# One root for the last two slabs of a two-layer graph network, and what is left on GpSimd at its end

## The chip, the cores and the metric

The kernel runs on one core of a Trainium2 chip. The metric is the time of one execution on the device in microseconds; a version is given by the median of its runs.

## The reference

The input is x (4096 x 64) and a sparse 0/1 matrix adj (4096 x 4096). Two graph layers follow one another, each inside a residual layer normalization:

```python
# layer 0: the last 100 neighbours of a row, each weighted by 0.5**(its rank from the end)
support = x @ weight
rank = jnp.cumsum(mask, axis=1); deg = rank[:, -1:]
k = jnp.minimum(deg, 100.); pos = rank - (deg - k)
w = mask * jnp.where(pos > 0, 0.5 ** (k - pos), 0.0)
x = _layernorm(x + w @ support + bias)

# layer 1: mean over neighbours and self, linear, relu, division by the row's length
deg = jnp.clip(jnp.sum(adj, axis=1, keepdims=True) + 1.0, 1.0, None)
z = jnp.concatenate([x, (adj @ x + x) / deg], axis=1) @ W + b
out = jax.nn.relu(z)
out = out / jnp.maximum(jnp.linalg.norm(out, axis=1, keepdims=True), 1e-12)
x = _layernorm(x + out)
```

`_layernorm` subtracts a row's mean and divides by sqrt(variance + 1e-5). That last division, in layer 1, is the place of the change.

## The kernel before, in words

**Tiles.** The 4096 rows are cut into eight slabs of 512 rows (g = 0 to 7; L = 7 is the last), and a slab into TB = 4 blocks of 128 rows, one row to a partition. A row statistic of a slab is a tile of 128x4, the rows' 64 features a tile of 128x256. The matrix comes in 64 pieces of 512 KB, loaded by GpSimd's DMA queue along with 16 smaller loads of x; SyncE's queue carries the weights and the eight stores of the result, one for each slab.

**Stages.** Up to about 205 us TensorE counts, weighs and sums layer 0 and, as soon as slabs of its result are there, sums parts of layer 1. From L756 on the order is written out by hand, call by call: the scheduler is manual, so each engine executes its instructions in the order in which the Python code emits them. The calls named `own` and `own_half` are what is left of TensorE's sums; the calls named `last_...`, `offset` and `store` are the epilogue of layer 1 for a unit of slabs (u6, u45, u01, u2, u3; the last slab comes in two halves u7b and u7a, and as u7 when they are joined).

**The epilogue of a unit**, in its order of data:

- `last_pz`, `last_z`, `last_relu`, `last_sq`, `last_ss`: the linear map, relu, and sums of squares;
- `last_rn` (with `last_sn` ahead of it for the halves of slab 7), `last_y`, `last_add`: division by the length and the residual;
- `last_mv`: mean and variance of each row (bn_stats and bn_aggr on VectorE);
- the root r = (variance + eps)^-0.5, in one of two forms. With a `last_s` ahead, `last_r` takes `root_b`: ScalarE has made s = sqrt(v + eps) (L358), VectorE refines it and inverts it with four small instructions (L364, L365, L367, L368). Without, `last_r` takes `root_p`: GpSimd adds eps (L376) and raises to -0.5 (L378);
- `offset`: off = -mean * r, on VectorE in one instruction (L735) for the first form, on GpSimd in two (L737, L738) for the second;
- `last_o`: y * r + off for each block of 128 rows, by ScalarE (L745, needs off), or (y - mean) * r by VectorE (L747, doesn't need off);
- `store`: SyncE's DMA (L754), which waits for the unit's normalizations.

Before the change only slab 7 has the first form. Slab 3's root and offset are GpSimd's last four instructions; slab 3's four blocks are normalized by ScalarE and stored, while slab 7's are shared: two by VectorE, two by ScalarE after slab 3's, and stored last. Slab 7's two halves write their moments into one tile, `mv_7` (128x4x2).

After the last instruction of each engine come closing ones that the kernel doesn't spell out: SyncE waits for the stores' semaphores, each engine executes a DRAIN, and a barrier over all engines (EVENT_SEMAPHORE) ends the program. The profile books them on L959, the line that builds the program.

Of the kernel before, what the change touches and what calls it, by code (L numbers as in the profile page):

```python
# [9 lines left out]
F32 = mybir.dt.float32  # L10
# [13 lines left out]
P = 128  # L24
R = 512
TB = R // P
# [13 lines left out]
def adj_resnorm_kernel(  # L40
# [23 lines left out]
    nc = tc.nc  # L64
# [11 lines left out]
    small = ctx.enter_context(tc.tile_pool(name="small", bufs=5))  # L76
# [276 lines left out]
    ep = {}  # L353

    def root_a(v, eps, name):

        s = small.tile([P, v.shape[1]], F32, tag="s", name=f"s_{name}")
        nc.scalar.activation(s, v, AF.Sqrt, bias=eps)  # L358
        return s

    def root_b(s, v, eps, name):

        q = small.tile([P, v.shape[1]], F32, tag="q", name=f"q_{name}")
        nc.vector.tensor_tensor(q, s, s, ALU.mult)  # L364
        nc.vector.scalar_tensor_tensor(q, q, eps, v, ALU.add, ALU.add)  # L365
        r = small.tile([P, v.shape[1]], F32, tag="r", name=f"r_{name}")
        nc.vector.reciprocal(q, q)  # L367
        nc.vector.scalar_tensor_tensor(r, s, 2.0, q, ALU.mult, ALU.mult)  # L368
        return r

    def root_p(v, eps, name, tag):

        n = v.shape[1]
        r = small.tile([P, n], F32, tag=tag, name=f"{tag}_{name}")
        if eps:
            nc.gpsimd.tensor_scalar(r, v, eps, None, ALU.add)  # L376
            v = r
        nc.gpsimd.tensor_tensor(r, v, power[:, 0:n], ALU.pow)  # L378
        return r

    def moments(y, name, mv=None):
        n = y.shape[1]
        st = small.tile([P, n, 6], F32, tag="st", name=f"st_{name}")
        if mv is None:
            mv = small.tile([P, n, 2], F32, tag="mv", name=f"mv_{name}")
        for t in range(n):
            nc.vector.bn_stats(st[:, t, :], y[:, t, :])
        for t in range(n):
            nc.vector.bn_aggr(mv[:, t, :], st[:, t, :])
        return mv  # L390
# [191 lines left out]
    L = NG - 1  # L582
# [55 lines left out]
    def unit(*slabs):  # L638
        name, bs = "_".join(map(str, slabs)), [g * TB + t for g in slabs for t in range(TB)]
        n = len(bs)  # L640
        tiles = []
        for i in range(n // TB):
            tiles.append(a16p.tile([P, 4 * TB // n, n, D], F32, tag="a16", name=f"u_{name}_{i}"))
        four = [t[:, i] for t in tiles for i in range(4 * TB // n)]
        return name, bs, four
# [51 lines left out]
    def last_y(u):  # L697
        name, bs, (z, _, y, _) = u
        rn = ep["rn", name].unsqueeze(2).to_broadcast([P, len(bs), D])
        nc.vector.scalar_tensor_tensor(y, z, 0.0, rn, ALU.max, ALU.mult)  # L700
# [3 lines left out]
        engine = nc.gpsimd if len(bs) >= TB else nc.vector  # L704
        engine.tensor_tensor(y, y, x1[:, rows(bs), :], ALU.add)

    mv_7 = small.tile([P, TB, 2], F32, tag="mv_7", name="mv_7")

    def last_mv(u):
        name, bs, (_, _, y, _) = u  # L710
        if len(bs) < TB:
            ep["mv1", str(L)] = mv_7
            t = bs[0] - L * TB
            moments(y, f"l1_{name}", mv_7[:, t : t + 2, :])
        else:
            ep["mv1", name] = moments(y, f"l1_{name}")

    def last_s(u):
        name = u[0]
        ep["s1", name] = root_a(ep["mv1", name][:, :, 1], eps_ln, f"l1_{name}")  # L720

    def last_r(u):
        name = u[0]
        v = ep["mv1", name][:, :, 1]
        if ("s1", name) in ep:
            ep["r1", name] = root_b(ep["s1", name], v, eps_ln, f"l1_{name}")
        else:
            ep["r1", name] = root_p(v, LN_EPS, name, "r1")

    def offset(u):  # L730
        name, bs, _ = u
        mv, r = ep["mv1", name], ep["r1", name]
        off = ep["off", name] = small.tile([P, len(bs)], F32, tag="off", name=f"off_{name}")
        if ("s1", name) in ep:
            nc.vector.scalar_tensor_tensor(off, mv[:, :, 0], -1.0, r, ALU.mult, ALU.mult)  # L735
        else:
            nc.gpsimd.tensor_tensor(off, mv[:, :, 0], r, ALU.mult)  # L737
            nc.gpsimd.tensor_scalar(off, off, -1.0, None, ALU.mult)  # L738

    def last_o(u, t0, t1, engine=nc.scalar):  # L740
        name, bs, (_, _, y, o) = u
        mv, r, off = ep["mv1", name], ep["r1", name], ep["off", name]
        for t in range(t0, t1):
            if engine is nc.scalar:
                engine.activation(o[:, t, :], y[:, t, :], AF.Identity, bias=off[:, t : t + 1], scale=r[:, t : t + 1])  # L745
            else:
                engine.tensor_scalar(  # L747
                    o[:, t, :], y[:, t, :], mv[:, t, 0:1], r[:, t : t + 1], ALU.subtract, ALU.mult
                )

    def store(u):
        name, bs, (_, _, _, o) = u
        for i, b in enumerate(range(0, len(bs), TB)):
            nc.sync.dma_start(out=out[bs[b] // TB], in_=o[:, b : b + TB, :])  # L754
# [46 lines left out]
    last_pz(u01)  # L801
    last_z(u45)
    last_mv(u6)
    last_relu(u45)
    last_sq(u45)
# [15 lines left out]
    u2 = unit(2)  # L821
    last_pz(u2)
    last_o(u6, 2, 4)
    last_o(u6, 0, 2)
    last_y(u45)
    last_rn(u01)
# [13 lines left out]
    own(3, 5)  # L840
    last_add(u01)
    last_mv(u45)
    own_half(1, 1)
    own_half(1, 4)
# [7 lines left out]
    u3 = unit(3)  # L852
    last_pz(u3)
    last_mv(u01)
    half_hT(1)
    u7 = unit(L)
# [14 lines left out]
    last_r(u01)  # L871
    own_half(0, 0)
    last_o(u45, 4, 6)
    last_ss(u3)
    own_half(0, 3)
# [27 lines left out]
    last_rn(u7a)  # L903
    offset(u2)
    last_o(u01, 6, 8)
    last_r(u3)
    last_y(u7a)
    last_add(u7a)
    last_o(u2, 0, 2)
# [1 line left out]
    last_mv(u7b)  # L911
    last_o(u2, 2, 4)
    last_mv(u7a)
    offset(u3)
    last_s(u7)
    store(u2)
    last_o(u3, 0, 2)
    last_r(u7)
    last_o(u3, 2, 4)
    offset(u7)  # L920
    last_o(u7, 2, 4, nc.vector)
    last_o(u7, 0, 2, nc.scalar)
    store(u3)
    store(u7)


_INS = ["x", "x_quads", "adjT", "weights"]
# [36 lines left out]
```

## Time and profile before

| what | us |
|---|---|
| time before, median of 3 runs (lowest, highest) | 243.77 (243.39, 243.98) |
| span of the profiled execution, first to last instruction | 241.5 |
| the runs' times less that span | 1.9 to 2.5 |
| TensorE busy in the span | 209.5 (87%) |
| VectorE busy | 175.7 (73%) |
| ScalarE busy | 135.4 (56%) |
| GpSimd busy | 92.8 (38%) |
| last ACTIVATE of ScalarE ends, from the span's start | 236.2 |
| last store issued | 236.25 |

The profile lists the span of the profiled execution, and no total for it apart from the runs' times; the last row but one and the last come from the timeline. A busy share is an average over the whole span, and in the last 10 us TensorE has nothing left to do, so the shares say little of the stage in which the change lies. The lines that matter are those of the timeline of that stage, of the chain of waits and of the closing instructions.

### The profile page before, as it was taken

Reading aid. Unit: us, or ns where it says so; the run is one execution under the profiler, and the core shown is the slowest. Engines: PE = TensorE matmul, PEld = TensorE weight load, DVE = VectorE, ACT = ScalarE, POOL = GpSimd, SP = SyncE. Lnnn points to the kernel's source line nnn. Section 1 sums busy time; section 2 is a strip of 40 time slices with the busy share of each in tenths; the row PEclk is TensorE's granted clock in tenths of the full one; section 3 lists DMA queues with packets and bytes.
Section 4 is the critical chain, followed back from the end, with each engine's and each line's share of the span. In section 5 each row is a group of like instructions: output and inputs, shape, how many; then the busy total and the mean of one; then the engine's idle time right before and its main releaser. Section 6 shows DMA issues by size and latency. Waiting matters only on the chain.

```text
span 241.5 us, 7394 instructions
## 1 busy us (share of the span) xinstructions
PE 209.5 (87%) x3123; PEld 95.2 (39%) x3167; DVE 175.7 (73%) x451; ACT 135.4 (56%) x203; POOL 92.8 (38%) x172
## 2 busy tenths in 40 slices
PE   8885679989699999999999999999999999996800
PEld 2222224333323442443345334433453454765700
DVE  5665677996488689579756975597559765789980
ACT  5375667787367647665555465555644521171691
POOL 8664588136106302133212421243161000287960
PEclk9999999999889999999999999999999999999975
DMA  5999999999999999999899999999970000000031
GB/s 92 185 227 247 247 224 210 216 225 213 212 226 214 212 217 220 212 214 216 145 174 176 196 184 185 186 191 188 197 146 3 3 0 0 3 18 6 0 109 43
DMA packets 11456, 37.33 MB, mean 155 GB/s; under 512 B 1568, under 2 KB 2720, under 8 KB 11424
## 3 DMA queue, kind: packets, MB, share of 16 engines
q0 software_dynamic: 9984, 35.66, 74.3%
q1 hardware_dynamic: 1440, 1.21, 1.5%
q8 instruction: 24, 0.39, 0.6%
q14 instruction: 8, 0.07, 0.1%
HBM read 69.37 MB, written 1.05 MB: 292 GB/s over the span
## 4 chain that ended last, share of the span: by engine, by line
PE 50%; DMA 21%; POOL 11%; DVE 8%; ACT 4%; issue 4%; POOLq 0%; ACTq 0%; DVEq 0%
PE acc L305 14%; PE acc_part L314 13%; DMA a<-in_adjT_dram 10%; PE v L278 6%; DMA x<-in_x_dram 6%; DMA c<-in_x_quads_dram 5%; PE cnt L248 4%; PE v L287 4%; ACT w L294 3%; POOL r L378 3%; POOL a L104 2%; PE va L314 2%; DVE w L295 2%; PE pz L414 2%; PE rep L266 1%
## 5 line engine op out<-in xcount | busy, mean ns | idle before, releaser
L294 ACT ACTIVATE w<-v,less 128x1024 int16<-128x1024 f32 x64 | 71.3, 1114 | 54.3 <-PE v L287 42.1
L295 DVE TENSOR_SCALAR w<-v 128x1024 int16<-128x1024 f32 x64 | 78.3, 1223 | 23.7 <-PE v L287 22.4
L305 PE MATMUL acc<-w,xhl 128*128 128x512 bf16 x236 | 66.0, 383 | 2.7 <-issue 1.4
L104 POOL DMA_DIRECT2D a<-in_adjT_dram x64 | 35.3, 554 | 80.3 <-PE acc_part L314 37.2
L314 PE MATMUL acc_part<-a,x1hl 128*128 128x512 bf16 x135 | 37.1, 381 | 1.9 <-issue 1.4
L305 PEld LDWEIGHTS <-xhl 128*128 128x128 f16 x256 | 23.1, 98 | 35.3 <-issue 11.5
L314 PEld LDWEIGHTS <-x1hl 128*128 128x128 f16 x224 | 18.6, 98 | 30.6 <-issue 13.4
L278 PE MATMUL v<-a,tri 32*32 32x512 bf16 x1024 | 29.5, 388 | 0.7 <-ACT w L294 0.6
L248 PE MATMUL cnt<-a,pick 128*32 128x512 bf16 x256 | 21.8, 387 | 8.6 <-DMA a<-in_adjT_dram 8.0
L258 DVE TENSOR_TENSOR cs<-cnt,cs 128x512 bf16<-128x512 f32 x27 | 18.5, 684 | 13.4 <-PE cnt L248 13.4
L287 PE MATMUL v<-near,mine 32*32 32x512 bf16 x1024 | 28.2, 379 | 0.0
L268 ACT ACTIVATE near<-rep,most 128x512 bf16<-128x512 f32 x35 | 23.9, 683 | 5.2 <-PE rep L266 5.1
L278 PEld LDWEIGHTS <-tri 32*32 32x32 bf16 x1024 | 9.8, 88 | 22.0 <-issue 21.3
L378 POOL TENSOR_TENSOR rn<-ss,power 128x4 f32<-128x4 f32 (+1 forms) x5 | 6.3, 1275 | 25.9 <-DVE ss L683 25.8
L266 PE MATMUL rep<-cs,further 128*128 128x512 bf16 x35 | 13.5, 386 | 1.9 <-DVE cs L258 1.5
L238 POOL TENSOR_TENSOR x<-x,wts 128x256 f32<-128x256 f32 x8 | 5.8, 728 | 24.3 <-DMA x<-in_x_dram 24.3
L248 PEld LDWEIGHTS <-pick 128*32 128x32 bf16 x256 | 5.0, 93 | 22.8 <-DMA a<-in_adjT_dram 12.6
L233 POOL TENSOR_TENSOR a<-a,ident_b 128x128 bf16<-128x128 bf16 x32 | 12.8, 433 | 0.1
L745 ACT ACTIVATE u<-u,off,r 128x64 f32<-128x64 f32 x28 | 10.0, 427 | 0.3 <-POOL off L738 0.3
L287 PEld LDWEIGHTS <-mine 32*32 32x32 bf16 x1024 | 9.7, 88 | 1.2 <-issue 1.0
L661 PE MATMUL va<-wts,hT 128*128 128x64 f32 x64 | 8.0, 276 | 2.4 <-DVE hT L629 1.9
L670 ACT ACTIVATE u<-u 128x256 f32<-128x256 f32 (+1 forms) x5 | 2.5, 502 | 12.4 <-DVE u L666 12.4
(136 smaller groups left out, 245.0 us busy)
## 6 DMA issues: line engine op xcount, KB each, us to landing
a<-in_adjT_dram POOLq DMA_DIRECT2D x64, 512.0 KB, 10.8
c<-in_x_quads_dram POOLq DMA_DIRECT2D x8, 128.0 KB, 11.6
x<-in_x_dram POOLq DMA_DIRECT2D x8, 128.0 KB, 8.6
out_dram<-u SPq DMA_DIRECT2D x8, 128.0 KB, 1.7
wts<-in_weights_dram SPq DMA_DIRECT2D x1, 160.0 KB, 7.4
touch<-in_x_quads_dram SPq DMA_DIRECT2D x1, 0.5 KB, 1.6
```

The source lines that it names most:

```text
L104: nc.gpsimd.dma_start(out=a, in_=adjT[g, k])
L248: nc.tensor.matmul(cnt[g][quarters[q], :], lhsT=pick[:, PW - 4 * k : PW - 4 * k + Q], rhs=A[g][k][:, q, :], start=first, stop=last,)
L258: nc.vector.tensor_tensor(new, cnt[g], cs[g], ALU.add)
L266: nc.tensor.matmul(pr, lhsT=further, rhs=cs[g], start=True, stop=True)
L268: nc.scalar.activation(near[g], pr, AF.Relu, bias=most, scale=-1.0)
L278: nc.tensor.matmul(v[e // 2][quarters[q], e % 2, :], lhsT=tri[quarters[e], :], rhs=A[g][k][quarters[e], q, :], start=True, stop=False,)
L287: nc.tensor.matmul(v[e // 2][quarters[q], e % 2, :], lhsT=mine[quarters[e], 4 * k + q, :], rhs=nr[quarters[e], :], start=False, stop=True,)
L294: nc.scalar.activation(w[:, 0:2, :], v[0], AF.Relu, bias=less)
L295: nc.vector.tensor_scalar(w[:, 2:4, :], v[1], -STEP * MAX_NEIGH, 0.0, ALU.add, ALU.max)
L305: nc.tensor.matmul(acc0[g], lhsT=xhl[:, b, :], rhs=w[:, q, :].bitcast(BF16), start=(k, q) == (NK - 1, 0), stop=(k, q) == (0, KB - 1),)
L314: nc.tensor.matmul(acc, lhsT=x1hl[:, b, :], rhs=A[g][b // KB][:, b % KB, :], start=first, stop=last)
L378: nc.gpsimd.tensor_tensor(r, v, power[:, 0:n], ALU.pow)
```

## The change

Slab 3's root is taken out of GpSimd and made together with slab 7's. `mv_7` becomes `mv_37`, with columns 0 to 3 for slab 3 and 4 to 7 for slab 7; a joint unit `u37` carries `last_s`, `last_r` and `offset` once over 128x8. Four GpSimd instructions (L376, L378, L737, L738 for slab 3) are gone. Each of the two slabs is then normalized half by VectorE and half by ScalarE, slab 7 ahead of slab 3, and stored in that order.

```diff
-    mv_7 = small.tile([P, TB, 2], F32, tag="mv_7", name="mv_7")
+    mv_37 = small.tile([P, 2 * TB, 2], F32, tag="mv_37", name="mv_37")
+    slot_of = {3: 0, L: TB}
 
     def last_mv(u):
         name, bs, (_, _, y, _) = u
-        if len(bs) < TB:
-            ep["mv1", str(L)] = mv_7
-            t = bs[0] - L * TB
-            moments(y, f"l1_{name}", mv_7[:, t : t + 2, :])
+        if bs[0] // TB in slot_of:
+            ep["mv1", "37"] = mv_37
+            t = slot_of[bs[0] // TB] + bs[0] % TB
+            moments(y, f"l1_{name}", mv_37[:, t : t + len(bs), :])
         else:
             ep["mv1", name] = moments(y, f"l1_{name}")
...
     def last_o(u, t0, t1, engine=nc.scalar):
         name, bs, (_, _, y, o) = u
-        mv, r, off = ep["mv1", name], ep["r1", name], ep["off", name]
+        if bs[0] // TB in slot_of:
+            n0 = slot_of[bs[0] // TB]
+            mv, r, off = [ep[what, "37"][:, n0 : n0 + TB] for what in ("mv1", "r1", "off")]
+        else:
+            mv, r, off = ep["mv1", name], ep["r1", name], ep["off", name]
...
     last_o(u01, 6, 8)
-    last_r(u3)
     last_y(u7a)
...
     last_mv(u7a)
-    offset(u3)
-    last_s(u7)
+    u37 = ("37", u3[1] + u7[1], None)
+    last_s(u37)
     store(u2)
-    last_o(u3, 0, 2)
-    last_r(u7)
-    last_o(u3, 2, 4)
-    offset(u7)
+    last_r(u37)
+    offset(u37)
     last_o(u7, 2, 4, nc.vector)
     last_o(u7, 0, 2, nc.scalar)
+    store(u7)
+    last_o(u3, 2, 4, nc.vector)
+    last_o(u3, 0, 2, nc.scalar)
     store(u3)
-    store(u7)
```

## The prediction

> **What bounds the kernel now.** I read the busy slices first, then the chain of waits, then the timeline of the last 10 us, and last the instructions of L959, the line that launches the program and to which its closing instructions are booked. The busy slices show TensorE at 0 in the last two of 40 (each 6.04 us), so from about 229 us the time belongs to the epilogue of layer 1. All instructions of the change lie there. The chain of waits runs through GpSimd until 234.10 (offset of slab 3), then ScalarE's normalizations to 236.22, and stops. The span ends at 241.5: 5.3 us after the last compute are not in that chain. The timeline shows both edges of the computation (columns: start, us, engine, line, operation, tiles, count):
>
> ```profile
> 232.13 0.23 POOL L376 TENSOR_SCALAR r<-mv_l 128x4 f32<-128x4 f32 x1
> 232.45 1.04 POOL L378 TENSOR_TENSOR r<-r,power 128x4 f32<-128x4 f32 x1
> 233.57 0.20 POOL L737 TENSOR_TENSOR off<-mv_l,r 128x4 f32<-128x4 f32 x1
> 233.78 0.30 ACT L358 ACTIVATE s_l<-mv,eps_ln 128x4 f32<-128x4 f32 x1
> 233.86 0.24 POOL L738 TENSOR_SCALAR off<-off 128x4 f32<-128x4 f32 x1
> 234.13 1.43 ACT L745 ACTIVATE u<-u,off,r 128x64 f32<-128x64 f32 x4
> 234.97 0.16 DVE L735 SCALAR_TENSOR_TENSOR off<-mv,r_l 128x4 f32<-128x4 f32 x1
> 235.05 0.53 DVE L747 TENSOR_SCALAR u<-u,mv,r_l 128x64 f32<-128x64 f32 x2
> 235.47 0.76 ACT L745 ACTIVATE u<-u,off,r_l 128x64 f32<-128x64 f32 x2
> ```
>
> ScalarE is ready at 234.08 (end of the root s_l) and GpSimd's offset at 234.10, so neither holds the other by more than 0.03 us. ScalarE ends at 235.47 + 0.76 = 236.23 and SyncE issues the last store at 236.25. What follows, from L959 in the windows 236.5 to 238.3, 238.3 to 239.5 and 240.7 to 240.9 (durations in ns: shortest/median/longest, then first and last start):
>
> ```profile
> L959 SPq EVENT_SEMAPHORE  x9: 17/28/28, 236.6 to 238.3; - x9
> L959 POOLq DRAIN  x1: 6902/6902/6902, 233.8 to 233.8; - x1
> ...
> L959 SPq DRAIN  x2: 7/7/7, 238.4 to 238.5; - x2
> ...
> L959 POOLq EVENT_SEMAPHORE  x2: 17/17/17, 240.8 to 240.8; - x2
> ```
>
> SyncE has waited for every store and is through at 238.46. Then nothing runs until 240.7 except one thing: GpSimd's closing DRAIN, begun at 233.81 (as GpSimd's last instruction was under way) and 6.90 us long, to 240.71. The closing barrier (GpSimd's EVENT_SEMAPHORE) starts 0.05 us later, and 0.75 us after that the span is over. **So the end is not set by the last store but by GpSimd: its last instruction ends at 234.10, plus 6.61 us of DRAIN.** SyncE has 2.25 us to spare.
>
> **What the Trainium skill says.** "Perfetto Trace Analysis", section "Sequencer-only Instruction (DRAIN, etc)", says that the profiler shows such an instruction from the moment its semaphores are satisfied; so the 6.90 us aren't a semaphore wait. The trace agrees in kind for ScalarE: its closing DRAIN starts at 235.2, takes 1.077 us and ends with its last ACTIVATE. "VectorE: DVE Perf Modes", section "The DRAIN you can't avoid", calls the closing DRAINs a constant of about 12 ns on all engines; this trace differs, 6902 ns on GpSimd, and the measurement decides. "DMA: Bandwidth & Descriptors", section "SWDGE vs HWDGE vs iDMA", says that DMAs issued from GpSimd have their descriptors made by software on its cores, and those from SyncE by hardware. All 80 loads here are GpSimd's (64 + 8 + 8 in the list of issues), all stores SyncE's. A tail that clears up after 80 DMAs would be 6.61 / 80 = 83 ns for each, my estimate from this trace; it would have nothing to do with the stores. No page gives its length.
>
> **The change part by part.**
>
> *GpSimd loses slab 3's root and offset:* L376 (0.23), L378 (1.04), L737 (0.20) and L738 (0.24), with gaps 232.06 to 234.10 = 2.04 us at the end of its queue. Nothing takes their place; its last instruction becomes slab 2's L738 (231.82 + 0.24 = 232.06). What comes before it is unmoved. With the DRAIN unchanged it ends at 232.06 + 6.61 = 238.67 in place of 240.71.
>
> *The root on ScalarE and VectorE becomes 128x8.* It replaces one of 128x4 at the same place in both queues and waits for the same last moments (slab 7, first half, done 233.75), since slab 3's moments are done by 231.47. ScalarE's Sqrt stays 233.78 to about 234.08. On VectorE five small instructions carry twice the columns. Nearest rows: L364 took 0.127 at 128x2 and 0.153 at 128x4, so about +0.05 for four columns more; L367 0.17 and 0.18, +0.02; L365 and L368 the same at both sizes, +0.01 each, and the offset +0.01. Sum +0.10. From below 0 (pipelining hides it), from above +0.25 (each grows as L364). I take +0.10: the offset ends at 235.13 + 0.10 = 235.23.
>
> *Order of the normalizations.* ScalarE did slab 3 (4) from 234.13 while VectorE made slab 7's root, then slab 7 (2). Now it has only 2 + 2 and all wait for the offset: it idles from 234.08 to 235.23 + 0.04 = 235.27 (0.04 is what passed from VectorE's ss_7a to ScalarE's root). Four ACTIVATEs start 0.34, 0.33 and 0.33 apart (six took 2.10 from 234.13 to 236.23), the last takes 0.42: end 236.70. Before: 236.23. **Price +0.47 us** on the way to the last store. VectorE's two added normalizations cost 2 x 0.22 and end at 235.15 + 3 x 0.22 + 0.31 = 236.12, before ScalarE; nothing is behind them.
>
> *Stores.* The same two DMAs in the other order. Slab 7's is issued when ScalarE has done its two, at 235.27 + 0.34 + 0.42 = 236.03, and occupies SyncE's queue for 0.33 (the duration of each issue) until 236.36; slab 3's follows at 236.72. They don't collide; before they stood at 235.59 and 236.25. Landing 1.7 us after issue (from the list of issues) is kept, so SyncE is through at 238.46 + 0.47 = 238.93.
>
> *VectorE and GpSimd's contention.* "SBUF — State Buffer", section "SBUF: two separate sides", says that GpSimd and VectorE share a port pair as an exclusive lock. The trace shows it: L677 at 128x128 took 0.757 while GpSimd's 128x256 add ran (229.29) and 0.292 otherwise. Does VectorE gain where GpSimd falls quiet, 232.06 to 234.10? Its L700 there took 0.292, as without GpSimd at 228.1: gain 0. In reverse the DRAIN now begins while VectorE still works, 4 us instead of 1.8; what that costs isn't shown; 0 to 1 us, I take 0 since its 6.9 us aren't tensor work, and keep 1 us for the range.
>
> *Sum.* The barrier starts after the later of GpSimd's DRAIN (238.67) and SyncE (238.93), plus about 0.05: 238.98 in place of 240.76. That is **-1.78 us**: 2.04 us freed on GpSimd, of which the last 0.26 are lost because the stores are late next. Span 241.50 - 1.78 = 239.72. The median shown, 243.77, stands 2.27 above the profiled span; I carry that over: **241.99, say 242.0 us**.
>
> **Rivals.**
>
> *The DRAIN has its fixed length after GpSimd's last instruction (forecast).* For: no semaphore wait in it, nothing else runs in its last 2.25 us, and ScalarE's and VectorE's DRAINs end with their own last work. Against: there is one such DRAIN in the trace, so a fixed length can't be told from a fixed end. 242.0; with 1 us more of DRAIN it ends at 239.67 and the time is 242.7. Chance 0.83.
>
> *The DRAIN ends with the stores.* It would last until a fixed time after the last store is in (240.71 - 238.46 = 2.25 after SyncE is through), whatever GpSimd did before. Then freeing GpSimd brings nothing and the late last store shows in full: +0.47, 244.2, slower by 0.19%, inside what can't be told from no change. It decides as soon as the DRAIN end moves with SyncE and not with GpSimd. Chance of this and of a DRAIN that grows to eat nearly all of the gain: 0.13.
>
> *The tail grows by more than the gain.* The same tie to the stores, with a root or a store that is later than worked out by 0.3 us or more: +0.25 from the root's upper bound, and VectorE slowed by the concurrent DRAIN. 244.6. For it: the 0.757 of L677. Against: VectorE's L735 and L747 already ran beside the DRAIN at 0.16 and 0.308, as L441's same shape elsewhere (0.307). Chance 0.04.
>
> That the change doesn't do what it says is no rival: GpSimd's list loses exactly the four instructions.
>
> **How the numbers follow.** A measurement here tells about 0.3% (0.73 us) from no change. The forecast's cases from -2.0 (root costs nothing and ScalarE starts sooner, so that the DRAIN alone decides: 238.67, -2.04) to -1.05 all lie beyond it: faster 0.83. Same 0.13, slower 0.04. Predicted 242.0. The range reaches from 241.5 (-2.04 and run-to-run 0.2) to 243.0 (the DRAIN 1 us longer and 0.3 of spread); the two tied cases are left out, together under 0.2.
>
> **What would show it.** Right: GpSimd's DRAIN starts near 231.8, lasts about 6.9 and ends near 238.7; the barrier starts right after SyncE's last DRAIN, near 238.9; ScalarE's last ACTIVATE ends near 236.7, 0.47 later than before. Wrong: a DRAIN that begins at 231.8 and still ends 2.2 us after SyncE's, so over 8.9 us long. The root's step is wrong if slab 7's offset ends after 235.4, the store's if the two issues stand within 0.4 us.

## The result, and the profile after

| | before | changed |
|---|---|---|
| median, us (22 runs each) | 243.69 | 242.34 |
| lowest, us | 242.75 | 241.33 |
| span of the profiled execution, us | 241.5 | 239.5 |

The ratio of the two is 0.9946, with a 95% interval of 0.9923 to 0.997: the changed kernel is faster by 0.5%, about 1.3 us.

The timeline of the changed kernel near its end (start, us, engine, line, operation):

```profile
231.64 0.24 POOL L739 TENSOR_SCALAR off<-off 128x4 f32<-128x4 f32 x1
...
233.28 0.30 DVE L389 BATCH_NORM_AGGREGATE mv<-st_l_7a 128x2 f32<-128x6 f32 x2
233.61 0.30 ACT L358 ACTIVATE s_l<-mv,eps_ln 128x8 f32<-128x8 f32 x1
233.94 0.17 DVE L364 TENSOR_TENSOR q_l<-s_l 128x8 f32<-128x8 f32 x1 [0.37 <-ACT s_l L358]
...
234.84 0.17 DVE L736 SCALAR_TENSOR_TENSOR off<-mv,r_l 128x8 f32<-128x8 f32 x1
234.93 0.98 DVE L752 TENSOR_SCALAR u<-u,mv,r_l 128x64 f32<-128x64 f32 x4
235.04 1.43 ACT L750 ACTIVATE u<-u,off,r_l 128x64 f32<-128x64 f32 x4 [1.13 <-DVE off L736]
```

GpSimd's last instruction is now slab 2's and ends at 231.88. ScalarE stands idle for 1.13 us behind the joint root's offset, which the last line shows in brackets, and ends at 235.04 + 1.43 = 236.48 (the times are rounded). The closing instructions, booked on L963 here, in the windows 236 to 238.3, 238.3 to 238.7 and 238.7 to 239.1:

```profile
L963 POOLq DRAIN  x1: 6902/6902/6902, 231.6 to 231.6; - x1
...
L963 SPq EVENT_SEMAPHORE  x6: 28/28/28, 238.3 to 238.6; - x6
...
L963 SPq DRAIN  x2: 7/7/7, 238.7 to 239.0; - x2
L963 POOLq EVENT_SEMAPHORE  x2: 17/17/17, 238.7 to 238.8; - x2
```

GpSimd's DRAIN has the same length to the nanosecond, 6902 ns, and ends at 238.50. SyncE is through at 238.72, and the barrier begins at 238.74, right behind it. The bound has moved from GpSimd's DRAIN to the last store.

To compare executions that reach the epilogue at different times, I use one zero from here on: **the end of VectorE's last bn_aggr (L389)**, the last moments of slab 7. "Tail" is the time from there to the end of the span. SyncE is "through" when the last DRAIN that it executes ahead of the barrier has ended; "barrier" is the start of GpSimd's first EVENT_SEMAPHORE behind its DRAIN. All times below are in us from that zero:

| | GpSimd's last instruction ends | DRAIN ends | ScalarE ends | SyncE through | barrier | tail |
|---|---|---|---|---|---|---|
| before | 0.35 | 6.97 | 2.48 | 4.71 | 7.01 | 7.76 |
| changed | -1.69 | 4.93 | 2.90 | 5.14 | 5.17 | 5.91 |

The barrier starts behind the later of DRAIN and SyncE, and the tail ends 0.75 after it. The tail is 1.85 us shorter. The spans differ by 2.0; the rest, 0.17 us, is that the zero itself came earlier in this execution (233.57 from the span's start, 233.74 before).

### The profile page after: what moved, and what is told of

Same layout as the page of the kernel before. It is cut to its first block, busy times and chain, and to the rows that moved or that the text cites. A ratio compares the mean times of both kernels' runs of the same rounds, so it can differ in the third digit from the quotient of the medians.

```text
span 239.5 us, 7390 instructions
## 1 busy us (share of the span) xinstructions
PE 208.1 (87%) x3123; PEld 95.3 (40%) x3167; DVE 176.7 (74%) x453; ACT 134.6 (56%) x201; POOL 91.4 (38%) x168
## 3 DMA queue, kind: packets, MB, share of 16 engines
q0 software_dynamic: 9984, 35.66, 75.6%
## 4 chain that ended last, share of the span: by engine, by line
PE 49%; DMA 24%; DVE 12%; POOL 7%; ACT 3%; issue 3%; ACTq 0%; POOLq 0%; DVEq 0%
DMA a<-in_adjT_dram 24%; PE acc L305 13%; PE acc_part L314 13%; PE v L278 6%; PE cnt L248 4%; PE v L287 4%; ACT w L294 2%; PE va L314 2%; POOL a L104 2%; PE pz L414 2%; DVE st_l L387 2%; DVE w L295 1%; DVE u L700 1%; PE va L661 1%; PE vb L314 1%
## 5 line engine op out<-in xcount | busy, mean ns | idle before, releaser
L305 PE MATMUL acc<-w,xhl 128*128 128x512 bf16 x236 | 65.3, 379 | 2.5 <-issue 1.3
L378 POOL TENSOR_TENSOR rn<-ss,power 128x4 f32<-128x4 f32 (+1 forms) x5 | 6.3, 1275 | 27.6 <-DVE ss L683 27.5
L661 PEld LDWEIGHTS va<-wts,hT 128*128 128x128 f32 x64 | 7.6, 191 | 3.7 <-DVE hT L629 2.8
```

What stands on the lines that cost most here:

```text
L305: nc.tensor.matmul(acc0[g], lhsT=xhl[:, b, :], rhs=w[:, q, :].bitcast(BF16), start=(k, q) == (NK - 1, 0), stop=(k, q) == (0, KB - 1),)
L661: nc.tensor.matmul(pz[:, t, :], lhsT=h[:, ts(b % TB, P)], rhs=wn_sb, start=True, stop=True)
```

## The experiments

Theory A: GpSimd's closing DRAIN has a length of its own after GpSimd's last instruction. Theory B: it ends with the stores.

### e1: GpSimd's four instructions put back, for nobody

```diff
     last_o(u01, 6, 8)
+    spare_r = root_p(mv_37[:, 0:TB, 1], LN_EPS, "spare", "r1")
     last_y(u7a)
...
+    spare_off = small.tile([P, TB], F32, tag="off", name="off_spare")
+    nc.gpsimd.tensor_tensor(spare_off, mv_37[:, 0:TB, 0], spare_r, ALU.mult)
+    nc.gpsimd.tensor_scalar(spare_off, spare_off, -1.0, None, ALU.mult)
     u37 = ("37", u3[1] + u7[1], None)
```

> The changed kernel with four GpSimd instructions put back at the old place and of the old shapes (add of eps, power, product, sign, 128x4), into tiles that nobody reads; ScalarE, VectorE and the stores stay as changed. Theory A (GpSimd's DRAIN has a fixed length after its last instruction): GpSimd ends about 2.0 us later, its DRAIN of 6.90 ends about 7.0 us after VectorE's last bn_aggr, the time from that bn_aggr to the end of the span goes from 5.91 back to 7.76, and the time to that of the kernel before, about 243.7. Theory B (the DRAIN ends with the stores): the DRAIN starts later and is 2 us shorter, the tail stays at 5.9, the time at about 242.3.

Measured: median 243.83 (20 runs), ratio to before 1.0 (0.9974 to 1.0025). **The whole gain is gone, though nothing reads the four results and ScalarE ends (2.90) and SyncE is through (5.14) just where they were in the changed kernel.** The last GpSimd line of its timeline, and its DRAINs (its L967; the long one is the third duration, starting at 234.5):

```profile
234.56 0.24 POOL L921 TENSOR_SCALAR off_spare<-off_spare 128x4 f32<-128x4 f32 x1
...
L967 POOLq DRAIN  x3: 46/102/6902, 234.5 to 241.9; - x3
```

Again 6902 ns. B is refuted: SyncE was through at 5.14, as in the changed kernel, and the barrier waited until 6.43, 0.05 behind the end of the DRAIN. The tail is 7.17, not the 7.76 that A gave, because GpSimd ended 0.24 before the zero and not 0.35 after it; that gap is taken up below, with e9a.

### e2: the kernel before, without slab 3's root

```diff
-    last_r(u3)
+    ep["r1", "3"] = ep["r1", "2"]
...
-    offset(u3)
+    ep["off", "3"] = ep["off", "2"]
```

> The kernel before, with slab 3's root and offset left out and slab 2's used in their place (slab 3's result is then not the reference's). GpSimd's four instructions are gone, ScalarE's and VectorE's order is that of before, so the joint root's price is not paid. Theory A: DRAIN 6.90 long, ending 4.9 us after the last bn_aggr; SyncE is through 4.7 after it, so the DRAIN is last again and the tail is about 5.7 (0.2 shorter than the changed kernel's 5.91); time about 1.9 to 2.0 below before. Theory B: SyncE is where it was, so the DRAIN ends where it did, tail 7.76, time as before.

Measured: median 242.05, ratio to before 0.9932 (0.9912 to 0.9953). That is 1.7 us below the kernel before, where 1.9 to 2.0 were expected. Taking GpSimd's four instructions away is enough for the gain, without the joint root. DRAIN 6901 ns. The tail is 5.32, not 5.7: GpSimd ended 2.87 before the zero, so its DRAIN (over at 3.75) was hidden and SyncE (4.55) decided. SyncE's 4.55 against the changed kernel's 5.14 is the price of the joint root and its order: 0.59 us.

### e3: what the DRAIN's length depends on

```diff
-        nc.gpsimd.dma_start(out=x1[:, ts(g, TB), :], in_=x[:, ts(g, TB), :])
+        nc.scalar.dma_start(out=x1[:, ts(g, TB), :], in_=x[:, ts(g, TB), :])
```

> The kernel before, with the eight loads of x (128 KB each) issued from ScalarE's queue at the same places in the code, so that GpSimd issues 72 DMAs in place of 80 and 3% fewer bytes; all arithmetic stays. It asks what the length of the DRAIN depends on. If it clears up after each DMA at the estimated 83 ns: DRAIN 6.90 - 8 x 0.083 = 6.24 us, the tail 7.76 - 0.66 = 7.10, time about 243.0. If it goes by bytes: 6.7 and 7.56. If it is constant: 6.90 and 7.76. In each case eight issues of some 0.3 us lie on ScalarE, which waits for TensorE there, and should cost nothing.

Its DRAINs, and those of e5, which issues 104 DMAs from GpSimd:

```profile
L959 POOLq DRAIN  x3: 46/93/6249, 234.5 to 241.2; - x3
```

```profile
L965 POOLq DRAIN  x3: 46/102/8862, 234.1 to 244.0; - x3
```

With 72 DMAs the DRAIN is 6249 ns and the tail 7.09: the per-DMA estimate said 6240 ns and 7.10. The barrier followed the DRAIN (6.30) by 0.04, with the stores where they were (SyncE 4.71): a second refutation of B. The time, 243.47 with a ratio of 0.9987 (0.996 to 1.0014), neither confirms nor excludes a gain of 0.66 us. The profiled execution reached the zero at 234.41, the one of before at 233.74; whether eight issues on ScalarE cost something earlier wasn't separated.

### e5: the same bytes in more DMAs

```diff
-            nc.gpsimd.dma_start(out=a, in_=adjT[g, k])
+            for j in range(2 if g > 4 else 1):
+                half = slice(2 * j, 2 * j + 2) if g > 4 else slice(0, KB)
+                nc.gpsimd.dma_start(out=a[:, half, :], in_=adjT[g, k][:, half, :])
```

> The changed kernel with each of the 24 matrix loads of slabs 5, 6 and 7 issued as two DMAs of half the size, so GpSimd issues 104 DMAs in place of 80 and the same bytes. It asks whether the DRAIN goes by the number of DMAs. From the DRAINs measured at 72, 74 and 80 DMAs (6.249, 6.412, 6.902 us) a line of 0.0816 us for each DMA: 6.902 + 24 x 0.0816 = 8.86 us at 104, of which the end of the span pays all but what SyncE still covers (0.2 us): tail 5.91 + 1.7 = 7.6 us. If it goes by bytes, or the loads of x were special, 6.90 and 5.91.

DRAIN 8862 ns, against 8.86 us expected. The length goes by the number of DMAs that GpSimd has issued and not by bytes. Packets (the pieces into which a DMA is cut, counted per queue in the profile) don't explain it either: e3 takes 384 of 9984 off GpSimd's queue and e5 adds 3456, nine times as many, and yet the DRAIN changes by 82 ns for each DMA in both.

| DMAs issued by GpSimd | 72 (e3) | 74 (e4) | 80 (before, changed) | 104 (e5) |
|---|---|---|---|---|
| DRAIN, ns | 6249 | 6412 | 6902 | 8862 |
| 368 + 81.67 x DMAs | 6248 | 6412 | 6902 | 8862 |

The tail expected was 7.6 and came out at 5.91, a miss: in this execution TensorE was granted half its clock for 6.8 us from 225 us on, the zero came at 238.38, and GpSimd was done 3.96 us ahead of it, so even 8.86 us of DRAIN were over (4.62) before SyncE (5.14). Its one time, 246.07, says little. So e5 shows the length of the DRAIN, and not what a longer one costs.

### e4 and e7: versions meant to beat both

e4, on the changed kernel:

```diff
+        queue = nc.gpsimd if g < 2 else nc.scalar
-        nc.gpsimd.dma_start(out=x1[:, ts(g, TB), :], in_=x[:, ts(g, TB), :])
+        queue.dma_start(out=x1[:, ts(g, TB), :], in_=x[:, ts(g, TB), :])
...
-    last_o(u3, 2, 4, nc.vector)
-    last_o(u3, 0, 2, nc.scalar)
+    last_o(u3, 1, 4, nc.vector)
+    last_o(u3, 0, 1, nc.scalar)
```

> The changed kernel with three further edits, a version meant to beat both: six of the eight loads of x (slabs 2 to 7) on ScalarE's queue, so 74 DMAs on GpSimd; slab 3's four normalizations split 3 to VectorE and 1 to ScalarE in place of 2 and 2; and, because the six loads take six of the rotating store semaphores, the last store gets the one for which SyncE waits last. Per-DMA theory: DRAIN 6.90 - 6 x 0.083 = 6.40, ending 4.43 us after the last bn_aggr. SyncE: 0.33 less from the split, some 0.36 less from the order of waits: through 5.14 - 0.69 = 4.45 after it. Tail about 5.2 in place of 5.91, time about 0.7 below the changed kernel. If the DRAIN is of constant length: it ends 4.93 after the bn_aggr, tail 5.7, time 0.2 below.

Median 242.13, ratio to before 0.9925 (0.9894 to 0.9955). DRAIN 6412 ns as expected; tail 5.34 where 5.2 was expected. ScalarE ended 0.33 earlier (2.57), but the last store went out only 0.23 earlier (2.70), since SyncE was busy with the store before it. SyncE was then through 0.15 us after the landing in place of 0.51: the order of its closing waits was worth its 0.36 us. The time was expected 0.7 us below the changed kernel's; the medians (242.13 and 242.34) differ by 0.2 and the intervals of the ratios overlap, so that e4 is the better one is read from the tails alone.

e7 has the last store issued by ScalarE besides:

```diff
+        queue = nc.scalar if name == "3" else nc.sync
-            nc.sync.dma_start(out=out[bs[b] // TB], in_=o[:, b : b + TB, :])
+            queue.dma_start(out=out[bs[b] // TB], in_=o[:, b : b + TB, :])
```

> The balanced version (74 DMAs on GpSimd, slab 3 split 3 to 1, last store on the semaphore waited for last) with the last store issued by ScalarE in place of SyncE. In the balanced version that store went out 0.13 us after ScalarE's last normalization, because SyncE was still busy with the store before it (two issues 0.435 us apart); from ScalarE's own queue it should go out within 0.04 us: about 0.1 us less than the balanced version's tail of 5.34, so 5.24, and the time 0.1 lower, which is less than a comparison of times tells; the tail in the profile decides. If an issue from ScalarE starts later or lands later than SyncE's 1.73 us, 5.3 or more.

Its last two stores in the timeline:

```profile
236.36 0.33 SPq L761 DMA_DIRECT2D out_dram<-u  x1
236.72 0.35 ACTq L761 DMA_DIRECT2D out_dram<-u  x1
```

They start 0.36 us apart in place of 0.44, the second 0.05 behind ScalarE's last normalization. GpSimd's DRAIN (over at 4.44) and SyncE (4.49) are about level now. Tail 5.26 (5.24 expected); median 241.72, ratio to before 0.9912 (0.9889 to 0.9935), the lowest of this study. Its interval overlaps the changed kernel's, so that it beats that one is read from the tails (5.26 against 5.91), not from the times.

### e6, e8 and e9: why the median moved less than the tail

The tails differ by 1.85 us, the medians by 1.35. Theory C: for 3.4 us, in some executions 6.8, the profile's clock column shows TensorE at half its clock (0.50 in place of 1.00); this interval falls at different places in different executions, and where it falls into the epilogue it takes part of the gain. The changed kernel again, beside e7:

> The changed kernel as it is, once more, beside the version e7. The median difference of the two kernels (1.35 us) is less than what the two profiles show in the tail (1.85 us). Theory C: an interval of about 3 us in which TensorE is granted half its clock falls near 223 to 227 us in many executions; it delays the last moments on VectorE by about 1.1 us but GpSimd hardly, so before the change, when GpSimd's end decided, it cost less (about 0.7, from the profile with the spare GpSimd work) than after it (1.1). If this profile has the interval there, the last bn_aggr ends near 234.7 in place of 233.6, GpSimd still ends near 231.9, the tail after the bn_aggr stays 5.91, and the span is about 240.6. Without the interval the span is 239.5 to 239.9. Median 241.9 to 242.4. Theory D (the change itself costs something ahead of the tail): bn_aggr late without such an interval.

Median 242.15 (6 runs), ratio to before 0.9933 (0.9909 to 0.9958). In this profile the interval lies at 65 to 68 us; zero at 233.89, tail 5.90, span 239.79. That says nothing for or against C, so four more profiles were taken:

> One more profile of the changed kernel, to see where the interval of half TensorE clock falls. Theory C in numbers, from the profiles so far: without the interval in 222 to 230 us GpSimd ends 1.69 us before the last bn_aggr and the span is 239.5 to 239.9; with it there (about 3 us long) GpSimd ends 2.87 before it, the last bn_aggr near 234.7, the tail still 5.91, the span about 240.6.

> As e8a: a second profile of the changed kernel, the same two alternatives.

> One more profile of the kernel before. Theory C: without the interval of half clock in 222 to 230 us GpSimd's last instruction ends 0.35 us after the last bn_aggr and the tail is 7.76, the span about 241.5; with it there GpSimd ends 0.24 before the last bn_aggr and the tail is 7.17, the span about 242.1: it loses 0.6 us less than the changed kernel, as in the profile with the spare GpSimd work.

> As e9a: a second profile of the kernel before, the same two alternatives.

Neither of e8's executions had the interval in the epilogue: spans 239.85 and 240.25, tails 5.91 both, GpSimd 1.69 before the zero both. Both of e9's had it. The stretches of the kernel before, in the first profile and then in e9a (columns: stretch, its length, busy time and count of PE, PEld, DVE, ACT, POOL, then the granted clock, DMA share, GB/s):

```profile
222.00:226.00 4.00, 3.15 (x29) 2.98 (x30) 3.90 (x28) 0.94 (x3) 3.40 (x6) 1.00 0.00 0
226.00:230.00 4.00, 2.55 (x22) 1.98 (x19) 3.75 (x20) 3.73 (x13) 3.83 (x5) 1.00 0.02 9
```

```profile
222.00:226.00 4.00, 3.22 (x21) 2.73 (x22) 3.90 (x27) 1.01 (x3) 3.43 (x7) 0.76 0.00 0
226.00:230.00 4.00, 3.54 (x26) 2.66 (x24) 2.85 (x17) 2.48 (x9) 3.81 (x5) 0.81 0.00 0
```

In e9a the clock column falls to 0.76 and 0.81, TensorE needs until 230.60 for what it had done by 229.04, and VectorE, which waits for TensorE, is busy 2.85 in place of 3.75 in the second stretch, while GpSimd stays at 3.81. So the last moments are late, and GpSimd's work on slabs finished earlier isn't. But GpSimd can get only so far ahead, for its last four instructions need slab 3's moments from VectorE. In e9a it stands idle for them, 0.66 us by the bracket:

```profile
232.21 0.36 DVE L389 BATCH_NORM_AGGREGATE mv_l<-st_l 128x2 f32<-128x6 f32 x4
...
232.65 0.23 POOL L376 TENSOR_SCALAR r<-mv_l 128x4 f32<-128x4 f32 x1 [0.66 <-DVE q_n_7a L364]
```

The bracket names VectorE's instruction right behind the moments, which ended 0.04 us after them. In the first profile the same L376 followed GpSimd's own work (231.82 + 0.24 = 232.06, start 232.13), 0.67 us after the moments. The executions side by side, in us from the zero:

| executions | interval in the epilogue | GpSimd ends | tail |
|---|---|---|---|
| before, first profile | no | 0.35 | 7.76 |
| before, e9a and e9b | yes | -0.23 | 7.18 |
| changed, first profile, e6, e8a, e8b | no | -1.69 | 5.90 to 5.91 |
| changed with split loads, e5 (interval of 7 us) | yes | -3.96 | 5.91 |

With GpSimd deciding, the tail absorbs 0.58 us of such a delay and no more: the moments of slab 3 end 2.28 us before the zero in every profile of the kernel before, and GpSimd's root and offset took 2.05 us from there in e9a, so GpSimd ends at -0.23 at the earliest. It stood there in e9b too, whose interval was 6.8 us long in place of e9a's 3.4 (its span, 243.5, was expected near 242.1). With SyncE deciding the tail absorbs nothing. Between two executions that both have the interval in the epilogue the tails differ by 7.18 - 5.91 = 1.27 us, without it by 1.85. That fits the 1.35 between the medians. It isn't fully shown: no profile of the unaltered changed kernel caught the interval there, and how often either kernel has it isn't counted. The spans of the changed kernel's 22 runs are a hint: 8 lie at 239.5 to 240.0, 8 at 240.4 to 241.1 and 6 at 242.0 to 242.5, where C expects 239.5 to 239.9 without the interval and about 240.6 with it; but a span doesn't say where an interval lay.

The traces also hint at what decides. The clock records change only in steps of 3.41 us, counted from the first moment of full clock (the 58.0 us up to an interval at 65 us are 17 steps, the 218.5 up to one at 224 are 64). TensorE has a pause of 1.92 us that begins between 220.7 and 222.7. In the six profiles with the interval in the epilogue (e1, e2, e4, e5, e9a, e9b) the whole pause lies in the step just ahead of it; in the other seven a step's border cuts the pause, in e8b by its last 0.02 us only, and there is no interval. The pause is there before and after the change alike. No run varied its place, so this is a pattern and not a shown cause, and the half clock at 65 us stays open.

Theory D isn't needed for the 1.35 us and isn't excluded: e8b's zero at 234.34, with no interval anywhere before it, is 0.77 later than the first profile's, and its cause stays open.

## Why the prediction was right

- **The bound.** The closing DRAIN set the end, and freeing GpSimd moved it: shown by e1 (four idle instructions restore the old time) and e2 (removing four is enough).
- **DRAIN unchanged, ending 2.04 us earlier.** Measured 6.97 to 4.93 from the zero: 2.04. The 0 to 1 us allowed for VectorE working beside it came out at 0: 6902 ns both times. The 83 ns for each DMA, an estimate from one DRAIN, measured 81.7, with 0.37 us independent of the count. (The DRAIN's record starts 0.05 us before that of GpSimd's last instruction, 233.81 and 233.86, and not while it was under way; the sum, which counts from that instruction's end, isn't touched.)
- **The root at 128x8, +0.10.** From the zero to the offset's end 1.39 before and 1.44 after: +0.04. It was mis-sized by 0.06; the five instructions grew by 2 to 24 ns each, the reciprocal most.
- **ScalarE's end and SyncE, +0.47.** Measured +0.43 for both, less by the root's 0.06. The stores stood 0.66 us apart as before (0.69 forecast) and didn't collide.
- **What is late next.** SyncE, as forecast: 0.22 us behind the DRAIN, 0.26 forecast.
- **Sum.** -1.78 in the barrier, measured -1.84 from the zero (7.01 to 5.17).
- **The reading that was wrong.** "Neither holds the other by more than 0.03 us", of ScalarE and GpSimd. The step took ScalarE to be free only when its root had ended. In e9a, where GpSimd was early, the next ACTIVATE started sooner and ScalarE ended at 2.32 and not 2.48: GpSimd had held it by 0.16. The change's true price on SyncE's path is therefore 5.14 - 4.56 = 0.58; 0.43 is what is left against an execution in which GpSimd's delay was in it.
- **A right value from a wrong reading.** VectorE's gain from a quiet GpSimd was put at 0 because L700 took 0.292 at 232.2 and "without GpSimd at 228.1". GpSimd's power (L378) ran from 227.67 to 228.68, so that row wasn't without it. In the changed kernel L700 did run with GpSimd quiet and took 0.293: the 0 was right, but by luck.
- **The term that was mis-sized.** The carry of the profiled difference to the median, -1.78 for -1.35. Both profiles had TensorE at full clock while it worked in the epilogue; with the interval there, the tails give 1.27. The forecast of 241.99 against 242.34 is off by these 0.43 us, less 0.08 because the median before was 243.69 over 22 runs and not 243.77. That the interval is the cause is likely and not fully shown (see above).
- **The rivals.** DRAIN tied to the stores: refuted by e1 and e3. Tail growing by more than the gain: in all profiles VectorE's 128x64 normalizations took 0.302 to 0.310 beside the DRAIN, and L441's, of the same shape, 0.307 without it.

## What to carry to other kernels

Look at what follows the last compute instruction: the chain of waits here stopped 5.3 us before the end of the span, and the closing instructions of the engines showed which one the others waited for. An engine with a long closing step should be the first to finish, even if another one then works a little later; the gain ends where the next engine (here the queue of the stores) takes over, and that can be read beforehand from when it was through. Compare two profiles from a common event inside the stage, not from the span's start, and look at the granted clock of that stage before carrying a difference to the median.

## What was not expected of the hardware

GpSimd's closing DRAIN grows by 81.7 ns for every DMA that GpSimd has issued in the program (72 to 104 were tried), though the last packet of its queue ends at 180.5 us and the DRAIN begins at 233.8; issuing loads from ScalarE's queue takes them out of it. What GpSimd does in that time isn't shown, nor whether an earlier DRAIN would take it off the end. And the order in which SyncE waits for the stores at the end is worth 0.36 us: each further wait took 0.06 us, and in the changed kernel six waits and two DRAINs stood behind the one for the last store.
